# Convolution taps of three groups as matrices on TensorE, and five tiles' spikes as signs on ScalarE

## The chip, the cores and the metric

The kernel runs on one core of a Trainium2 chip. A core has TensorE (PE in the profile, its weight loads PEld), VectorE (DVE), ScalarE (ACT), GpSimdE (POOL) and SyncE (SP, which here issues the DMAs). TensorE writes its results to PSUM; the other operands lie in SBUF. The metric is device microseconds of one execution; smaller is better.

## The reference

The input is x, 16 sequences of 64 tokens with 256 features (1024 token rows), and a context of 16 x 1601 x 256. Six residual sublayers follow each other, each on a layer-normed x:

1. cross-attention over the context;
2. a selective state-space layer ("SSM"): in-projection, a causal convolution of four taps per channel, SiLU, projections to a step size delta and to b and c, a recurrence over the 64 tokens for 512 channels x 16 states, a gate, out-projection;
3. a spiking feed-forward layer;
4. windowed cross-attention over the context's first 64 rows;
5. a self-attention with a distance threshold;
6. a mixture of 8 experts with two chosen per token.

The change touches two places. The convolution, one filter of four taps for each of the 512 channels:

```python
xc = lax.conv_general_dilated(xc, conv_w, window_strides=(1,), padding=[(D_CONV - 1, 0)],
    dimension_numbers=('NCH', 'OIH', 'NCH'), feature_group_count=D_INNER)
xc = xc + conv_b[None, :, None]
x_b = jax.nn.silu(jnp.transpose(xc, (0, 2, 1)))
```

and the spikes of the feed-forward layer, five steps of a leaky integrator fed with the same y:

```python
reset = jax.lax.stop_gradient(spike_fn(mem - THRESHOLD))
mem_new = BETA * mem + y - reset * THRESHOLD
spk = spike_fn(mem_new - THRESHOLD)
...
return jnp.sum(spks, axis=0) / NUM_STEPS
```

Since y is the same in all steps, the number of spikes is a step function of y: it is the number of five thresholds (`SPIKES`, lines 110 to 136) that y lies above.

## The kernel before

The 1024 token rows are 8 tiles of 128 (two sequences each). Everything is float32.

The first part, sublayer 1 (`l0_cross`, line 545), goes through the tiles one after the other and reads the context: scores (line 609), exponentials, transposed weights (646, 651), weighted values (654).

The SSM goes by five groups of tiles, `GROUPS = [(0, 1), (1, 2), (3, 2), (5, 2), (7, 1)]`: first tile and number of tiles, so groups 0 and 4 have T = 128 token columns and groups 1, 2 and 3 have T = 256. It has two halves. `l0_ssm_prelude` (line 736) works with channels on the partitions: layer norm, then `project` for pairs of 128-channel chunks. For the first four chunks the in-projection lands in a PSUM bank, ScalarE writes it with its bias into a padded buffer `xpad` (line 776) and, times the last tap, into `ug` (line 782), and VectorE adds the three earlier taps, one instruction each (line 787). For the other four chunks (the gate) ScalarE only adds the bias (766). Then come SiLU (807, with a table load before and after it), x_proj (819), and in two halves the step size: dt matmuls (840), a softplus of several ScalarE, VectorE and GpSimd steps (846 to 866). delta, delta*u and b, c are written to DRAM (824, 868), from where `l0_ssm_state` reads them back spread over the partitions (893, 904).

`l0_ssm_state` (line 884) does 16 steps for a group, 80 in all: four ScalarE exponentials `decay` (922, two buffers), then on VectorE a product (942), a scan (943) and a product (944), then four TensorE matmuls with the matrix `fold` that sum over states (948). After each four steps comes a product with the gate (953), at the end the out-projection (`so_ps`) and its residual (373). Steps are counted here from 1 to 80 in program order: group 0 has steps 1 to 16, group 1 17 to 32, group 2 33 to 48, group 3 49 to 64, group 4 65 to 80.

The later sublayers go tile by tile in `later` (1649): `l0_ffn` (1028: fc and pj matmuls at the helper lines 438 and 448, spikes), `l1_cross` (1119), `l1_self` (1233), `l1_moe` (1398: hidden matmuls `he_ps`, outputs `eo_ps`, and on VectorE one weighted accumulation per expert at 1469). They run on streams with their own buffers and PSUM banks and overlap with the SSM of later tiles. Stream 3 and the preludes of groups 3 and 4 (`banks[: 1 if g >= P2 else 2]`, line 1560) share the PSUM bank "p".

For the spikes, `l0_ffn` copies the projection out of PSUM on ScalarE (1059), then VectorE compares it with the first threshold (1060) and adds the comparison with each of the four others (1062); the residual adds 0.2 times the count.

The order on each engine is fixed when the program is built: a list scheduler (`schedule_with_timeline_sim=True`, with costs from `scheduler_costs`, line 146) issues what its own model holds ready, by priority. Priorities come from offsets in the table `AT` (line 87), one for each block: 'C' for the cross-attention tiles, 'P' for the preludes, 'S' for the state halves, 'D' for the later sublayers of each tile, 'W' for weight loads. `HOLD = {4: (2, 2)}` keeps group 4's state half behind the self-attention of tile 2. Each engine then runs its list strictly in order.

Of the kernel before, what the change touches and what calls it, by code (L numbers as in the profile page):

```python
# [11 lines left out]
F32 = mybir.dt.float32  # L12
# [86 lines left out]
PB = 8  # L99
PADX, PADR, PADC, SPLD, SPLM = 1, 1, 1, 1, 1  # L100
VPV = 0
PAIR = 0
LNA = tuple(range(8))
ST1 = 1
# [114 lines left out]
def kernel(ctx: ExitStack, tc: tile.TileContext, a: dict, out: bass.AP):  # L219
# [486 lines left out]
    def l0_ssm_setup(w, pool, late):  # L706
        A.activation(w["am"], w["am"], AF.Exp)
        V.tensor_scalar(w["am"], w["am"], -1.0, None, ALU.mult)
        if CONV:
            w["taps"] = pool.tile([P, NE * DCONV, P], F32, name="taps")  # L710
            for c in range(NE):
                for t in range(DCONV):
                    V.tensor_scalar(
                        w["taps"][:, c * DCONV + t, :], ident, w["conv_w"][:, c, t : t + 1],
                        None, ALU.mult,
                    )

        w["b3"] = pool.tile([P, NE], F32, name="b3")
        V.tensor_mul(w["b3"], w["conv_w"][:, :, DCONV - 1], w["in_b"][:, 0:NE])
        V.tensor_add(w["b3"], w["b3"], w["conv_b"])  # L720
        w["xpad"] = []
        for k in range(2):
            t = pool.tile([P, GT // L, XP], F32, name=f"xpad{k}")
            G.memset(t, 0.0)
            w["xpad"].append(t)
        if DSK:
            w["Dd"] = late.tile([P, NE, P], F32, name="Dd")
            for c in range(NE):
                A.activation(w["Dd"][:, c, :], ident, AF.Copy, scale=w["D"][:, c : c + 1])
        w["decay"] = []  # L730
        for k in range(NDEC):
            t = late.tile([P, 4 * GT], F32, name=f"decay{k}")
            G.memset(t, 0.0)
            w["decay"].append(t)

    def l0_ssm_prelude(w, pp, late, banks, g):
# [22 lines left out]
        def project(oc):  # L759
            ps = bank("in_ps", [P, 2, T])  # L760
            for k in range(2):
                pe[g, "in", oc + k] = mm_T(ps[:, k, :], w["in_w"], hT, oc + k)
            if oc >= NE:
                for k in range(2):
                    c = oc + k
                    A.activation(
                        ug[:, c, :], ps[:, k, :], AF.Identity, bias=w["in_b"][:, c : c + 1]
                    )
                return
            xps = []  # L770
            for k in range(2):
                c = oc + k
                xp = w["xpad"][k][:, 0:nb, :]
                xps.append(xp)
                pv = ps[:, k, :].rearrange("p (b l) -> p b l", l=L)
                A.activation(
                    xp[:, :, DCONV - 1 :], pv, AF.Identity, bias=w["in_b"][:, c : c + 1]
                )
                if CONV:
                    continue  # L780
                cv = ug[:, c, :].rearrange("p (b l) -> p b l", l=L)
                A.activation(  # L782
                    cv, pv, AF.Identity, bias=w["b3"][:, c : c + 1],
                    scale=w["conv_w"][:, c, DCONV - 1 : DCONV],
                )
                for t in range(DCONV - 1):
                    V.scalar_tensor_tensor(  # L787
                        cv, xp[:, :, t : t + L], w["conv_w"][:, c, t : t + 1], cv,
                        ALU.mult, ALU.add,
                    )  # L790
# [32 lines left out]
        s["bc"] = dram.tile([2 * DST, T], F32, name=f"d_bc{g}")  # L823
        nc.sync.dma_start(out=s["bc"], in_=dbl[DTR:DBL, :])

        if split and not GLAST:
            for oc in range(NE, 2 * NE, 2):
                project(oc)


        s["delta"] = dram.tile([DIN, T], F32, name=f"d_delta{g}")
        s["du"] = dram.tile([DIN, T], F32, name=f"d_du{g}")
        for hf in range(2):
            shp = [P, 2, T]
            ps = bank("dt_ps", shp)
            e = sized(pp, "spe", 2, T)
            vp = sized(pp, "spv", 2, T, bufs=2)
            for k in range(2):
                c = 2 * hf + k
                pe[g, "dt", hf] = nc.tensor.matmul(  # L840
                    ps[:, k, :], w["dt_w"][:, c * P : (c + 1) * P], dbl if PADX else dbl[0:DTR, :],
                    start=True, stop=True,
                )
            for k in range(2):
# [21 lines left out]
            V.tensor_mul(du, vp, ug[:, 2 * hf : 2 * hf + 2, :])  # L866
            for k, t in (("delta", vp), ("du", du)):
                nc.sync.dma_start(
                    out=s[k].rearrange("(c p) t -> p c t", p=P)[:, 2 * hf : 2 * hf + 2, :],
                    in_=t,  # L870
                )
        if split:
            if GLAST:
                for oc in range(NE, 2 * NE, 2):
                    project(oc)
            with tc.issue_after(sp_last.ins) if SAFT else nullcontext():
                silu(ug[:, NE:, :])
        return s

    turns = [0]  # L880
# [3 lines left out]
    def l0_ssm_state(w, pp, s, g):  # L884
# [2 lines left out]
        x = xs[g]  # L887
        bc = []
        for q in range(2):
            t = sized(pp, f"bc{q}", 4, T)  # L890
            src = s["bc"][q * DST : (q + 1) * DST, :].rearrange("(k n) t -> n k t", n=SN)
            for n in range(SN):
                nc.sync.dma_start(
                    out=t[n * SD : (n + 1) * SD, :, :], in_=src[n].partition_broadcast(SD)
                )
            bc.append(t)
        yg = sized(pp, "yg", NE, T)
        for c in range(NE):
            rep = {}
            for k in ("delta", "du"):  # L900
                t = sized(pp, "rep_" + k, 4, T, bufs=REPB)
                src = s[k][c * P : (c + 1) * P, :].rearrange("(k d) t -> d k t", d=SD)
# [125 lines left out]
    def l0_ffn(w, st, i0):  # L1028
# [779 lines left out]
```

## Time and profile before

| | |
|---|---|
| median of 3 runs | 719.25 us (718.08 to 721.94) |
| the profiled execution | 717.57 us, span 715.5 us, mean granted TensorE clock 0.943 |
| TensorE busy | 616.6 us (86%) |
| VectorE busy | 520.0 us (73%) |
| ScalarE busy | 478.8 us (67%) |
| GpSimdE busy | 211.6 us (30%) |
| data moved by DMA | 102.56 MB |

Shares over the whole span hide that the stages have different limits. The first scan starts at 107.7 us; up to there TensorE and the DMA queues carry the cross-attention. Then VectorE carries the state steps, and from about 500 us on TensorE has hardly a gap. So times are read here by stretch: busy time of each engine between two events. A group of the profile (a "row") is all instructions of one line, operation and tile shape; it gives the busy time, the number and the mean duration. One float32 matmul of the program shows as two TensorE instructions in the profile.

### The profile page before, as it was taken

How to read it: one execution, taken by the hardware profiler on the slowest of the kernel's cores; microseconds unless marked ns; L12 is line 12 of the kernel's file. 1: busy time of each engine (PE TensorE's matmuls, PEld its weight loads, DVE VectorE, ACT ScalarE, POOL GpSimd, SP SyncE). 2: the span in 40 equal slices, each digit the busy share in tenths (PEclk: the TensorE clock that was granted, in tenths of full speed). 3: DMA queues.
4: the chain of work that ended last, by engine and by line, in shares of the span. 5: the costliest groups of instructions: out<-in, count | busy, mean ns of one | idle time of the engine just before them, and what ended most of it. 6: DMA issues, size and time to landing. Idle time of an engine off the chain costs nothing.

```text
span 715.5 us, 13023 instructions
## 1 busy us (share of the span) xinstructions
PE 616.6 (86%) x4508; PEld 436.3 (61%) x4508; DVE 520.0 (73%) x876; ACT 478.8 (67%) x1570; POOL 211.6 (30%) x300
## 2 busy tenths in 40 slices
PE   9988969989997487786786869789998989999997
PEld 7455545544653265553453647656787777878986
DVE  3424328896999999999999679999879944433432
ACT  3444536965677366797789667768977788674442
POOL 4110110130011579012226592522326533221100
PEclk9999998989999599899788789999999999999999
DMA  8999689799942954211113301255554540000000
GB/s 301 325 372 335 211 276 327 216 383 289 295 123 74 308 134 98 60 33 59 60 31 97 105 30 41 66 146 156 154 148 117 154 159 9 1 1 1 17 14 8
DMA packets 85383, 102.56 MB, mean 143 GB/s; under 512 B 11515, under 2 KB 67763, under 8 KB 85190
## 3 DMA queue, kind: packets, MB, share of 16 engines
q1 hardware_dynamic: 85318, 101.74, 46.2%
q8 instruction: 36, 0.59, 0.4%
q14 instruction: 29, 0.24, 0.1%
HBM read 96.33 MB, written 5.37 MB: 142 GB/s over the span
## 4 chain that ended last, share of the span: by engine, by line
PE 43%; DVE 24%; DMA 13%; ACT 8%; issue 6%; POOL 4%; SPq 2%; DVEq 0%; POOLq 0%; ACTq 0%
PE he_ps L438 7%; DVE hs L943 7%; PE eo_ps L448 6%; PE s_ps L609 6%; DVE hs L942 5%; DVE hs L944 4%; PE o_ps L654 4%; PE in_ps L438 3%; DMA w<-in_L_ffn_w 3%; ACT decay L922 2%; DMA rep_delta<-d_delta 2%; PE fc_ps L438 2%; DMA Wv<-in_L_attn_Wv 1%; DMA cT<-in_ctxT 1%; PE qk_ps L438 1%
## 5 line engine op out<-in xcount | busy, mean ns | idle before, releaser
L943 DVE TENSOR_TENSOR_SCAN hs<-decay,hs 128x1024 f32<-128x1024 f32 (+1 forms) x80 | 155.1, 1949 | 0.2
L922 ACT ACTIVATE decay<-rep_delta,ssm 128x252 f32<-128x252 f32 (+1 forms) x320 | 122.2, 458 | 37.8 <-DVE hs L943 30.5
L942 DVE TENSOR_TENSOR hs<-rep_du,bc 128x1024 f32<-128x1024 f32 (+1 forms) x80 | 87.9, 1106 | 14.1 <-PE y_ps L948 6.4
L944 DVE TENSOR_TENSOR hs<-hs,bc 128x1024 f32<-128x1024 f32 (+1 forms) x80 | 87.5, 1101 | 0.1
L948 PE MATMUL y_ps<-hs,fold 128*32 128x256 f32 (+1 forms) x640 | 45.3, 367 | 14.2 <-DVE hs L944 14.1
L609 PE MATMUL s_ps<-cT,qkT 128*64 128x512 f32 (+1 forms) x256 | 54.3, 509 | 0.4 <-ACT qkT L499 0.3
L1469 DVE SCALAR_TENSOR_TENSOR x<-eo_ps,pad,x 128x256 f32<-128x256 f32 x56 | 26.8, 478 | 37.5 <-PE eo_ps L448 37.4
L654 PE MATMUL o_ps<-cn,prT 128*64 128x256 f32 x384 | 51.0, 402 | 2.7 <-ACT prT L651 2.7
L1458 ACT ACTIVATE he<-he_ps,late 128x128 f32<-128x128 f32 x112 | 35.2, 366 | 24.7 <-PE he_ps L438 24.3
L1167 POOL TENSOR_TENSOR ke<-kT,hmask 128x512 f32<-128x512 f32 x28 | 45.7, 1651 | 15.7 <-PE s_ps L1172 15.2
L654 PEld LDWEIGHTS o_ps<-cn,prT 128*64 128x64 f32 x384 | 28.4, 144 | 21.4 <-ACT prT L651 5.9
L438 PE MATMUL in_ps<-hT,L_attn_in_proj_wT 128*128 128x256 f32 (+1 forms) x160 | 35.7, 374 | 5.9 <-ACT hT L432 4.6
L948 PEld LDWEIGHTS y_ps<-hs,fold 128*32 128x32 f32 x640 | 15.0, 112 | 35.7 <-DVE hs L944 21.6
L651 ACT COPY prT<-prT_ps 128x512 f32<-128x512 f32 (+1 forms) x32 | 16.1, 505 | 29.8 <-PE prT_ps L646 29.6
L438 PEld LDWEIGHTS in_ps<-hT,L_attn_in_proj_wT 128*128 128x128 f32 x160 | 28.3, 214 | 12.3 <-ACT hT L432 4.7
L1179 ACT ACTIVATE sm<-s_ps,wmx 128x64 f32<-128x64 f32 x112 | 33.6, 322 | 3.2 <-DVE wmx L1176 3.1
L438 PE MATMUL fc_ps<-hT,L_ffn_W_fcT 128*128 128x128 f32 x224 | 29.9, 284 | 6.2 <-ACT hT L432 6.2
L438 PEld LDWEIGHTS fc_ps<-hT,L_ffn_W_fcT 128*128 128x128 f32 x224 | 27.8, 196 | 8.9 <-ACT hT L432 7.3
L438 PE MATMUL he_ps<-hT,w 128*128 128x128 f32 x192 | 27.3, 284 | 6.4 <-DMA w<-in_L_ffn_w 3.9
L627 POOL TENSOR_TENSOR xnb<-xmx,qb 128x1 f32<-128x1 f32 x8 | 2.7, 334 | 101.4 <-DVE xmx L616 88.1
L787 DVE SCALAR_TENSOR_TENSOR ug<-xpad,ssm,ug 128x256 f32<-128x256 f32 (+1 forms) x60 | 26.2, 461 | 8.2 <-ACT ug L782 7.8
L609 PEld LDWEIGHTS s_ps<-cT,qkT 128*64 128x64 f32 x256 | 17.0, 136 | 23.8 <-issue 18.4
(406 smaller groups left out, 1495.2 us busy)
## 6 DMA issues: line engine op xcount, KB each, us to landing
cn<-in_ctx SPq DMA_DIRECT2D x48, 512.0 KB
cT<-in_ctxT SPq DMA_DIRECT2D x42, 512.0 KB
w<-in_L_ffn_w SPq DMA_DIRECT2D x48, 256.0 KB
rep_delta<-d_delta SPq DMA_DIRECT2D x48, 128.0 KB
rep_du<-d_du SPq DMA_DIRECT2D x48, 128.0 KB
bc<-d_bc SPq DMA_DIRECT2D x24, 128.0 KB
rep_delta<-d_delta SPq DMA_DIRECT2D x32, 64.0 KB
rep_du<-d_du SPq DMA_DIRECT2D x32, 64.0 KB
```

What stands on the lines that cost most here:

```text
L438: last = nc.tensor.matmul(ps, w[:, kc, oc * P : (oc + 1) * P], src[:, kc, :], start=(kc == 0), stop=(kc == nk - 1),)
L448: nc.tensor.matmul(ps, srcT[:, kc, j * P : (j + 1) * P], w[:, kc, :], start=(kc == 0), stop=(kc == nk - 1),)
L609: nc.tensor.matmul(s_ps[r * L : (r + 1) * L, :n], q["qkT"][:, kc, r * L : (r + 1) * L], cT[r][:, kc, :], start=(kc == 0), stop=(kc == KC - 1),
L654: q["last"] = nc.tensor.matmul(q["o"][r * L : (r + 1) * L, :], prT[:n, j % 4, r * L : (r + 1) * L], cn[r, j], start=(j == 0), stop=(j == NKB),
L922: A.activation(dav[:, (4 * j + k) * nb : (4 * j + k + 1) * nb, 1:], rep["delta"][:, k, :].rearrange("p (b l) -> p b l", l=L)[:, :, 1:], AF ...
L942: V.tensor_mul(hv, dv, bv)
L943: V.tensor_tensor_scan(hf, da, hf, 0.0, ALU.mult, ALU.add)
L944: V.tensor_mul(hv, hv, cv)
L948: nc.tensor.matmul(y_ps[k * SD : (k + 1) * SD, :], fold, hs[:, 4 * j + k, :], start=(m0 + j == 0 and not DSK), stop=(m0 + j == NG - 1),)
L1167: G.tensor_mul(ke, kT[:, c, tok].unsqueeze(1).to_broadcast([P, HPC, L]), hmask.unsqueeze(2).to_broadcast([P, HPC, L]),)
L1179: A.activation(sm[:, k, :], s_ps[:, k, :], AF.Exp, bias=nmx[:, k : k + 1], accum_out=su[i][:, c * HPC + k : c * HPC + k + 1],)
L1458: A.activation(he[:, oc, :], ps[:, oc, :], AF.Relu, bias=w["b1"][:, e * KC + oc : e * KC + oc + 1],)
```

## The change

- `CVG = (2, 3, 4)`: in these groups' preludes line 782 and the three VectorE taps of line 787 are left out. Instead ScalarE builds four 128x128 matrices for each chunk, the identity times one tap's column of weights (48 instructions in all; they lie in the buffers `spe` and `spd` of the softplus), TensorE multiplies them with four shifted views of `xpad` and sums in a bank `cv_ps` (48 matmuls), and ScalarE writes that with the convolution's bias into `ug`.
- `SPKA = (0, 1, 2, 3, 4)`: for these tiles the copy and the five VectorE instructions are left out. ScalarE takes the sign of y minus each threshold as bfloat16 straight from PSUM (5 instructions), TensorE adds the five signs and a half with the identity (6 matmuls in bfloat16), and ScalarE turns the sum into a whole count in two instructions, adding and subtracting 3 * 2**22.
- Constants for this: 8 GpSimd memsets near the start.
- All offsets in `AT` are replaced.
- `PR = ()` brings a further variant that is not used (no group is in it). A DMA of `bc` is put behind that condition and otherwise unchanged.

```diff
-AT = {'C': [-2353, 5581, 7142, -5613, 8966, 8274, 4756, 5756], 'P': [8396, -16035, 6317, -7280, -4284], 'S': [-14451, -3588, 2275, 4502, 10207], 'D': [1074, 3097, 6442, 3653, 3047, 2495, 11233, 1972, 3894, 14390, 5543, -1098, -3696, 8030, 8748, 8626, 4822, -6980, 6568, -2434, 5400, 13909, -16420, 15355, 10997, 6273, 17387, 6006, 5142, 8066, 4192, 8614], 'W': [22978, 1143]}
+AT = {'C': [-5139, 6805, 7005, -2417, 3697, 7786, 3506, 9074], 'P': [7946, -18619, 10584, -6550, -1170], 'S': [-13797, -4499, 733, 6029, 9327], 'D': [1201, 2427, 8508, 2754, 4728, 3096, 9632, 3223, 5211, 22017, 5232, -2472, -6148, 9346, 9404, 9102, 4452, -7971, 6779, -1693, 3783, 14663, -19173, 10370, 11088, 4756, 17922, 6455, 6997, 8294, -28, 9918], 'W': [14796, -151]}
...
+CVG = (2, 3, 4)
+SPKA = (0, 1, 2, 3, 4)
+PR = ()
...
+    c_spk = cpool.tile([P, len(SPIKES)], F32, name="c_spk")
+    for k, v in enumerate(SPIKES):
+        G.memset(c_spk[:, k : k + 1], -v)
+    c_rnd = cpool.tile([P, 2], F32, name="c_rnd")
+    G.memset(c_rnd[:, 0:1], 2.0 + 3.0 * 2**22)
+    G.memset(c_rnd[:, 1:2], -3.0 * 2**22)
+    halfb = cpool.tile([P, 1], BF16, name="halfb")
+    G.memset(halfb, 0.5)
...
-                if CONV:
+                if CONV or g in CVG:
                     continue
...
+            if g in CVG:
+                ps = bank("cv_ps", [P, 2, T])
+                for k in range(2):
+                    taps = sized(pp, ("spe", "spd")[k], DCONV, P, most=P)
+                    for t in range(DCONV):
+                        A.activation(
+                            taps[:, t, :], ident, AF.Copy,
+                            scale=w["conv_w"][:, oc + k, t : t + 1],
+                        )
+                    for t in range(DCONV):
+                        nc.tensor.matmul(
+                            ps[:, k, :], taps[:, t, :], xps[k][:, :, t : t + L],
+                            start=(t == 0), stop=(t == DCONV - 1),
+                        )
+                for k in range(2):
+                    c = oc + k
+                    A.activation(
+                        ug[:, c, :], ps[:, k, :], AF.Identity, bias=w["conv_b"][:, c : c + 1]
+                    )
...
-        if i0 in SPKB:
+        if i0 in SPKA:
+
+
+            sums = st.bank("spk_ps", shp)
+            for k, v in enumerate(SPIKES):
+                r = st.new("r", [P, nt * D // 2]).bitcast(BF16).rearrange("p (n d) -> p n d", n=nt)
+                A.activation(r, ps, AF.Sign, bias=c_spk[:, k : k + 1])
+                nc.tensor.matmul(sums, identb, r, start=(k == 0), stop=False)
+            nc.tensor.matmul(
+                sums, identb, halfb.unsqueeze(1).to_broadcast(shp), start=False, stop=True
+            )
+            total = st.new("total", shp)
+            A.activation(total, sums, AF.Identity, bias=c_rnd[:, 0:1], scale=0.5)
+            A.activation(total, total, AF.Identity, bias=c_rnd[:, 1:2])
+        elif i0 in SPKB:
```

The lists of instructions that the build gives differ, besides the order, only by these numbers: VectorE has 36 taps and 25 spike instructions fewer; ScalarE has 48 taps, 25 signs and 10 rounding steps more and 5 copies fewer (12 instructions of line 782 become 12 of the new bias line); TensorE has 48 float32 and 30 bfloat16 matmuls more; GpSimd has 8 memsets more. The DMAs are the same, in another order.

More of the change, by code (lines that the diff above doesn't have):

```diff
@@ L729, in l0_ssm_setup @@
                 A.activation(w["Dd"][:, c, :], ident, AF.Copy, scale=w["D"][:, c : c + 1])
+        if PR:
+            t = late.tile([P, 4 * GT], F32, tag="bc0", name="seld")
+            w["bc0"] = t[:, 0 : 4 * P].rearrange("p (k t) -> p k t", k=4)
+            w["seld"] = t[:, 4 * P :].rearrange("p (k t) -> p k t", k=4)
+            w["selb"] = sized(late, "hs", 8, P, bufs=HSB, most=P)
+            for j in range(4):
+                G.tensor_copy(
+                    w["seld"][:, j, :].rearrange("p (n d) -> p n d", d=SD),
+                    ident[:, j * SD : (j + 1) * SD].unsqueeze(1).to_broadcast([P, SN, SD]),
+                )
+            for k in range(8):
+                r = DTR + k * SN
+                G.tensor_copy(
+                    w["selb"][:, k, :].rearrange("p (n d) -> p n d", d=SD),
+                    ident[:, r : r + SN].unsqueeze(2).to_broadcast([P, SN, SD]),
+                )
         w["decay"] = []
@@ L789, in project @@
                         ALU.mult, ALU.add,
+                    )
[12 more added lines that the diff above has]
+                            start=(t == 0), stop=(t == DCONV - 1),
+                        )
+                for k in range(2):
+                    c = oc + k
+                    A.activation(
+                        ug[:, c, :], ps[:, k, :], AF.Identity, bias=w["conv_b"][:, c : c + 1]
                     )
@@ L822, in l0_ssm_prelude @@
         A.copy(dbl, ps)
-        s["bc"] = dram.tile([2 * DST, T], F32, name=f"d_bc{g}")
-        nc.sync.dma_start(out=s["bc"], in_=dbl[DTR:DBL, :])
+        if g not in PR:
+            s["bc"] = dram.tile([2 * DST, T], F32, name=f"d_bc{g}")
+            nc.sync.dma_start(out=s["bc"], in_=dbl[DTR:DBL, :])
         if split and not GLAST:
@@ L828, in l0_ssm_prelude @@
                 project(oc)
-        s["delta"] = dram.tile([DIN, T], F32, name=f"d_delta{g}")
-        s["du"] = dram.tile([DIN, T], F32, name=f"d_du{g}")
+        s["rep"] = []
+        if g not in PR:
+            s["delta"] = dram.tile([DIN, T], F32, name=f"d_delta{g}")
+            s["du"] = dram.tile([DIN, T], F32, name=f"d_du{g}")
         for hf in range(2):
@@ L866, in l0_ssm_prelude @@
             V.tensor_mul(du, vp, ug[:, 2 * hf : 2 * hf + 2, :])
+            if g in PR:
+                s["rep"] += [(vp[:, k, :], du[:, k, :]) for k in range(2)]
+                continue
             for k, t in (("delta", vp), ("du", du)):
@@ L877, in l0_ssm_prelude @@
                 silu(ug[:, NE:, :])
+        if g in PR:
+            s["bc"] = []
+            for q in range(2):
+                t = sized(late, "bc1", 4, T) if q else w["bc0"]
+                ps = bank("bc_ps", [P, 4, T])
+                for k in range(4):
+                    nc.tensor.matmul(
+                        ps[:, k, :], w["selb"][:, q * 4 + k, :],
+                        dbl, start=True, stop=True,
+                    )
+                A.copy(t, ps)
+                s["bc"].append(t)
+        s["bank"] = bank
         return s
@@ L889, in l0_ssm_state @@
         for q in range(2):
+            if g in PR:
+                bc.append(s["bc"][q])
+                continue
             t = sized(pp, f"bc{q}", 4, T)
@@ L901, in l0_ssm_state @@
                 t = sized(pp, "rep_" + k, 4, T, bufs=REPB)
+                if g in PR:
+                    ps = s["bank"]("rep_ps", [P, 4, T])
+                    for j in range(4):
+                        nc.tensor.matmul(
+                            ps[:, j, :],
+                            w["seld"][:, j, :],
+                            s["rep"][c][k == "du"], start=True, stop=True,
+                        )
+                    A.copy(t, ps)
+                    rep[k] = t
+                    continue
                 src = s[k][c * P : (c + 1) * P, :].rearrange("(k d) t -> d k t", d=SD)
@@ L1043, in l0_ffn @@
         shp = [P, nt, D]
-        if i0 in SPKB:
+        if i0 in SPKA:
[4 more added lines that the diff above has]
+                nc.tensor.matmul(sums, identb, r, start=(k == 0), stop=False)
+            nc.tensor.matmul(
+                sums, identb, halfb.unsqueeze(1).to_broadcast(shp), start=False, stop=True
+            )
+            total = st.new("total", shp)
+            A.activation(total, sums, AF.Identity, bias=c_rnd[:, 0:1], scale=0.5)
+            A.activation(total, total, AF.Identity, bias=c_rnd[:, 1:2])
+        elif i0 in SPKB:
             y = st.new("y", shp)
```

## The prediction

> **What bounds the kernel now.** I read the busy slices first, then busy times by stretch, then VectorE's rows and waits, then the order of the instructions.
>
> ```profile
> PE   9988969989997487786786869789998989999997
> DVE  3424328896999999999999679999879944433432
> ACT  3444536965677366797789667768977788674442
> PEclk9999998989999599899788789999999999999999
> ```
>
> VectorE is full from about 180 to 500 us; TensorE has gaps there and none behind. Two events part the stretches: the first scan (107.7 us) and the scan of step 61 (480.9 us), whose fold matmuls end at 489.8 us.
>
> ```profile
> 0.00:107.70 107.70, 93.55 (x630) 59.04 (x630) 35.79 (x109) 47.35 (x122) 17.62 (x62) 0.97 0.91 303
> 107.70:480.90 373.20, 299.90 (x2115) 193.95 (x2119) 346.41 (x467) 271.14 (x813) 130.42 (x131) 0.90 0.48 142
> 480.90:715.50 234.60, 223.13 (x1767) 183.27 (x1759) 137.84 (x303) 160.28 (x638) 63.60 (x108) 1.00 0.25 73
> 489.80:715.50 225.70, 214.99 (x1706) 178.53 (x1706) 128.94 (x288) 153.83 (x612) 62.45 (x105) 1.00 0.24 71
> ```
>
> Columns after the length: busy TensorE, weight loads, VectorE, ScalarE, GpSimd, then TensorE's clock. In the second stretch VectorE is idle for 26.8 us, TensorE for 73.3, ScalarE for 102.1: VectorE sets its length. Behind step 61 TensorE is idle for 10.7 of 225.7 us: TensorE sets the end. What VectorE is spared therefore pays only by letting this dense part begin earlier, and whatever TensorE is given to do there comes off.
>
> VectorE's rows that the change takes from, and its waits in the second stretch:
>
> ```profile
> L787 DVE SCALAR_TENSOR_TENSOR ug<-xpad,ssm,ug 128x256 f32<-128x256 f32 x36 | 17.6, 506 | 1.9 <-ACT ug L782 1.7
> L787 DVE SCALAR_TENSOR_TENSOR ug<-xpad,ssm,ug 128x128 f32<-128x128 f32 x24 | 8.6, 393 | 6.3 <-ACT ug L782 6.2
> L1062 DVE SCALAR_TENSOR_TENSOR total<-y,total 128x256 f32<-128x256 f32 x28 | 14.8, 529 | 0.1
> L1060 DVE TENSOR_SCALAR total<-y 128x256 f32<-128x256 f32 x7 | 2.8, 405 | 1.7 <-ACT f L1038 1.0 <-ACT y L1059 0.8
> ```
>
> ```profile
> DVE hs L942 <- DMA rep_delta<-d_delta: 6.0, 1, 6.0
> DVE hs L942 <- PE y_ps L948: 4.7, 4, 2.7
> DVE few L1362 <- ACT sm L1357: 4.1, 1, 4.1
> DVE ug L787 <- ACT ug L782: 1.7, 1, 1.7
> DVE total L1060 <- ACT f L1038: 1.0, 1, 1.0
> ```
>
> **The change, part by part.** I price by a row's busy time over its number.
>
> *VectorE, second stretch.* Removed: 24 taps at 17.6/36 = 0.489 us (11.7), 12 at 8.6/24 = 0.358 (4.3), 20 comparisons at 14.8/28 = 0.529 (10.6), 5 at 0.4 (2.0): 28.6 us. The new order moves more: adding row prices over VectorE's list from the first scan to that of step 61 gives 378.1 us before and 336.4 after, 41.7 less. So 13.1 us of other work (four expert accumulations of line 1469, residuals, small steps of the self-attention) now stand behind step 61. Rows overlap: 378.1 stand for 346.4 busy, so 336.4 stand for 308.2.
>
> *Waits.* Of 26.8 us idle, 1.7 and 1.0 belong to removed instructions. 4.1 is a reciprocal for which VectorE waits on ScalarE at 406 to 410 us; in the new list a gate product, two products and a scan stand between the reduction ahead of it and that reciprocal, which cover the wait. I leave 20.0. Ends: 0 (no wait left) and 53.6 (twice the row, ScalarE and TensorE both being fuller); I take 20.0, since the four large waits that stay have causes that are untouched. Step 61's scan then starts at 107.7 + 308.2 + 20.0 = 435.9 instead of 480.9, its folds end at 444.8.
>
> *TensorE ahead of step 61.*
>
> ```profile
> L438 PE MATMUL in_ps<-hT,L_attn_in_proj_wT 128*128 128x256 f32 x96 | 25.3, 412 | 5.3 <-ACT hT L432 4.6 <-ACT ug L782 0.6
> L438 PE MATMUL in_ps<-hT,L_attn_in_proj_wT 128*128 128x128 f32 x64 | 10.5, 318 | 0.6 <-ACT ug L782 0.6
> L1158 PE MATMUL s_ps<-cneg,identb 128*64 128x512 bf16 x32 | 6.7, 415 | 0.7 <-DVE qu L1136 0.7
> ```
>
> A float32 matmul is two records: 25.3/48 = 0.527 us and 10.5/32 = 0.328. The taps cost 32 x 0.527 + 16 x 0.328 = 22.1 us, all ahead of step 61. A bfloat16 spike matmul of half the row's width lies between 0.1 and 0.21 (half the row, the row); 30 cost 3.1 to 6.3, I take 3.1, as matmul rows here shrink with width. Yet TensorE's list ahead of step 61's folds, from the first fold on, falls from 317 to 298 us of row prices: at the old ratio to busy (299.8/317) 282 us in some 329, 86% against 80%. The 22.1 us are hidden by TensorE's idle time; without that cover they come on top.
>
> *TensorE behind step 61.* Instead of 910 matmuls 1062 follow: 32 more expert hidden and 14 output matmuls, 12 fc, 10 pj, 12 for spikes and the attention of later tiles. By rows 263 become 311 us; 263 stood for 215.0 busy, so 311 stand for 254.1, 39.1 more. Nothing hides these. Idle stays 10.7.
>
> *ScalarE.*
>
> ```profile
> L729 ACT ACTIVATE Dd<-ident,ssm x4: 385/386/388, 38.2 to 39.1; 128x128 f32<-128x128 f32 x4
> L766 ACT ACTIVATE ug<-in_ps,ssm 128x256 f32<-128x256 f32 x12 | 5.0, 469 | 5.8 <-PE in_ps L438 5.8
> ```
>
> 48 taps at 0.386 are 18.5 us; 25 signs and 10 rounding steps at 0.469 are 16.4; five copies go (-1.9), line 782's successor is cheaper (-1.1): 31.9 us. ScalarE's list up to step 61 stays at 294 us of rows, since other work moves behind it: 271 busy in 328 instead of 373, 83% instead of 73%. I price this at nothing on the path, covered by its idle time; without cover it is the second rival. Both lists have 11 table loads (1.283 us each in the profile), so the signs bring none.
>
> [...]
>
> *The rest.* Eight memsets (0.1 us in their row's size) come early on GpSimd; the loads of the context (3.7 to 10.5 us) and x (10.5 to 17.2) cover them, else +0.8. In groups 3 and 4 the single bank "p" now holds also the taps' sums, 8 x 0.527 = 4.2 us more per pair; the prelude of group 3 spent 282 to 306 us, mostly queued behind scans, so this is no longer than before. The DMAs are the same number; in SP's list group 2's writes of delta and du and its first reads now stand ahead of the feed-forward weights. Those were issued from 232 us on and fc began at 297, so they can wait for some tens of us.
>
> *Sum.* 444.8 + 254.1 + 10.7 = 709.6 us span, 2.1 around it: **711.7, say 712**, against 717.57 of the profiled execution (its median is 1.7 above). VectorE gives 45, TensorE's longer list takes 39.
>
> **The rivals.**
>
> *Faster still (700).* VectorE's waits go to 8 and nothing else changes. For: 200 to 400 us had 4 us of waits in all. Against: the waits on DMA (6.0) and on folds (4.7) have untouched causes.
>
> *Slower: ScalarE is late with the decays (726).* Between the scans ScalarE's queue now holds runs of eight taps (3.1 us, six of them) and of five signs with two roundings (3.3 us, three tiles ahead of step 61): 28.4 us, each in front of some decay that has only two buffers. If VectorE waits for half, step 61 comes 14 us later and the end at 726. It decides from 9.5 us of such waits on (721). For: ScalarE rises to 83%. Against: decays waited 30.5 us for scans, so ScalarE was ahead.
>
> *Slower: group 2's round trip (722).* By rows there are 19 us between the last product of its first half and step 33 (42 before); the slowest trip in the chain of waits took 18 us (147.1 to 165.4). A queue in front, like the 10.6 us of a weight load there, makes step 33 late by 10. Against: these weights now go behind it.
>
> *No gain (718).* TensorE can't do 282 us of mixed work in 329, and step 61 is 6 us later. Against: the 282 are counted at the old stretch's clock of 0.90, and behind 490 us it is 1.00.
>
> [...]
>
> **How the numbers follow.** My sum 0.50 (own range 704 to 720), 700 0.18, ScalarE's lateness 0.18, the round trip 0.06, no gain 0.08. The ends of the waits give 692 and 745. Below 697 VectorE would have to wait for under 5 us in all, above 730 for over 38; a tenth each, so 697 to 730. Under 0.5% (3.6 us) this kernel can't be told from unchanged: from 714 to 721 is the same. Of my sum 0.31 is faster, 0.14 the same, 0.05 slower; with the rest faster 0.50, same 0.24, slower 0.26.
>
> **What would show it.** Right: the 61st scan near 436 us, VectorE's idle time from the first scan to it near 20, TensorE busy some 254 of 265 us behind its folds, he_ps and eo_ps among them. Wrong: large waits of hs (943) on decay (922); a wait of line 942 on DMA before step 33; TensorE idle more than 20 us behind step 61; taps or signs far from 0.386 and 0.469.

## The result and the profile after

The changed kernel takes 741.85 us (median; 740.91 to 742.60), the kernel before 718.92 in the same series: a ratio of 1.031 [1.028, 1.034], slower by 3%. 712 was forecast, with 697 to 730 as the range; the time lies outside it and on the other side. The profiled execution took 742.03 us with a span of 740.3. In the table of the experiments one execution each of both_old and both_pfree, in which the chip was in a slower state, is left out of the median and the ratio.

The busy slices of the changed kernel:

```profile
PE   9998999769896878977997867899998999999997
DVE  2433369598799895899999996845889225334332
```

The stretches in the form of the table of before (length; busy time of TensorE, weight loads, VectorE, ScalarE, GpSimd; granted clock), from the first scan (101.4 us) to the scan of step 61 (459.1), and from the end of step 61's folds (467.0) to the end:

```profile
101.40:459.10 357.70, 293.69 (x1999) 189.61 (x1996) 311.65 (x361) 264.44 (x774) 107.93 (x108) 0.87 0.49 145
467.00:740.30 273.30, 257.72 (x1988) 212.87 (x1986) 135.42 (x336) 184.41 (x732) 66.47 (x128) 0.99 0.24 72
```

Step 61 comes 21.8 us earlier than before (480.9), not 45. The part behind its folds grows from 225.7 to 273.3 us. The difference of the spans is 467.0 - 489.8 + 273.3 - 225.7 = 24.8 us. In the first stretch VectorE's idle time is 357.70 - 311.65 = 46.05 us, where 20 were forecast and 26.8 stood before. TensorE is busy there for 82%, with gaps.

VectorE's largest waits in that stretch, and the rows of the new operations:

```profile
DVE hs L1024 <- PE y_ps L1030: 11.5, 7, 4.4
DVE diff L1406 <- POOL few L1398: 5.9, 1, 5.9
DVE yg L1035 <- PE y_ps L1030: 5.0, 4, 3.7
DVE hs L1024 <- DMA bc<-d_bc: 5.0, 1, 5.0
DVE hs L1024 <- DMA rep_du<-d_du: 4.7, 2, 4.5
```

```profile
L1133 ACT ACTIVATE r<-pj_ps,c_spk 128x256 bf16<-128x256 f32 x25 | 9.8, 491 | 1.7 <-PE pj_ps L460 1.7
L825 ACT ACTIVATE spe<-ident,ssm 128x128 f32<-128x128 f32 x24 | 7.6, 389 | 2.0 <-PE cv_ps L830 2.0
L830 PE MATMUL cv_ps<-xpad,spd 128*128 128x256 f32 x32 | 7.9, 383 | 0.0
L1134 PE MATMUL spk_ps<-r,identb 128*128 128x256 bf16 x25 | 4.9, 272 | 1.9 <-ACT r L1133 1.3
```

Of the kernel before, the prediction shows the products' wait for folds (`y_ps`), 4.7 us, but not that of the product with the gate:

```profile
DVE yg L953 <- PE y_ps L948: 3.5, 1, 3.5
```

The waits for folds have grown from these 4.7 and 3.5 us to 11.5 and 5.0; none is a wait of a scan or product for a decay. The rows of matrices, signs and tap matmuls are close to the prices of the prediction (a float32 tap matmul, two records, takes 7.9/16 = 0.494 us for 0.527). The bfloat16 spike matmul is not: 4.9/25 = 0.196 us, where 0.1 was taken.

### The profile page after: what moved, and what is told of

Same layout as the page of the kernel before. It is cut to its first block, busy times and chain, and to the rows that moved or that the text cites. A ratio compares the mean times of both kernels' runs of the same rounds, so it can differ in the third digit from the quotient of the medians.

```text
span 740.3 us, 13311 instructions
## 1 busy us (share of the span) xinstructions
PE 650.9 (88%) x4634; PEld 465.8 (63%) x4634; DVE 490.7 (66%) x815; ACT 501.8 (68%) x1648; POOL 193.8 (26%) x308
## 5 line engine op out<-in xcount | busy, mean ns | idle before, releaser
L1025 DVE TENSOR_TENSOR_SCAN hs<-decay,hs 128x1024 f32<-128x1024 f32 (+1 forms) x80 | 152.6, 1913 | 1.1
L666 PE MATMUL o_ps<-cn,prT 128*64 128x256 f32 x384 | 54.9, 407 | 5.7 <-ACT prT L663 5.7
L1030 PE MATMUL y_ps<-hs,fold 128*32 128x256 f32 (+1 forms) x640 | 48.7, 381 | 10.6 <-DVE hs L1026 10.6
L1263 POOL TENSOR_TENSOR ke<-kT,hmask 128x512 f32<-128x512 f32 x28 | 41.1, 1489 | 21.0 <-PE s_ps L1268 20.7
L666 PEld LDWEIGHTS o_ps<-cn,prT 128*64 128x64 f32 x384 | 30.7, 143 | 22.5 <-ACT prT L663 7.9
L450 PE MATMUL fc_ps<-hT,L_ffn_W_fcT 128*128 128x128 f32 x224 | 34.8, 304 | 0.8 <-ACT f L1120 0.5
L450 PEld LDWEIGHTS fc_ps<-hT,L_ffn_W_fcT 128*128 128x128 f32 x224 | 31.9, 216 | 5.4 <-issue 1.3
L621 PEld LDWEIGHTS s_ps<-cT,qkT 128*64 128x64 f32 x256 | 17.9, 139 | 26.8 <-issue 21.4
L639 POOL TENSOR_TENSOR xnb<-xmx,qb 128x1 f32<-128x1 f32 x8 | 4.6, 578 | 106.5 <-DVE xmx L628 58.4
L460 PE MATMUL pj_ps<-L_ffn_W_projT,f 128*128 128x256 f32 x112 | 28.6, 400 | 2.0 <-ACT f L1121 1.0
```

The lines of the kernel that those rows point to most:

```text
L450: last = nc.tensor.matmul(ps, w[:, kc, oc * P : (oc + 1) * P], src[:, kc, :], start=(kc == 0), stop=(kc == nk - 1),)
L460: nc.tensor.matmul(ps, srcT[:, kc, j * P : (j + 1) * P], w[:, kc, :], start=(kc == 0), stop=(kc == nk - 1),)
L621: nc.tensor.matmul(s_ps[r * L : (r + 1) * L, :n], q["qkT"][:, kc, r * L : (r + 1) * L], cT[r][:, kc, :], start=(kc == 0), stop=(kc == KC - 1),
L666: q["last"] = nc.tensor.matmul(q["o"][r * L : (r + 1) * L, :], prT[:n, j % 4, r * L : (r + 1) * L], cn[r, j], start=(j == 0), stop=(j == NKB),
L1025: V.tensor_tensor_scan(hf, da, hf, 0.0, ALU.mult, ALU.add)
L1030: nc.tensor.matmul(y_ps[k * SD : (k + 1) * SD, :], fold, hs[:, 4 * j + k, :], start=(m0 + j == 0 and not DSK), stop=(m0 + j == NG - 1),)
```

## The experiments

Steps are counted as before. In the expectations, "operations", "offsets" and "order" are three theories of the loss: the added instructions, the particular offsets of the new `AT`, or any list that the scheduler makes anew. All ratios are to the kernel before, run on the same chip in turn with each kernel.

| kernel | median, us | ratio [95%] |
|---|---|---|
| none_old | 764.83 | 1.063 [1.058, 1.067] |
| none_new | 764.23 | 1.062 [1.058, 1.066] |
| both_old | 755.54 | 1.049 [1.044, 1.053] |
| taps_old | 777.89 | 1.078 [1.072, 1.084] |
| none_held | 718.50 | 0.999 [0.996, 1.002] |
| both_held | 732.62 | 1.020 [1.016, 1.025] |
| taps_held | 737.51 | 1.028 [1.023, 1.032] |
| signs_held | 715.24 | 0.996 [0.994, 0.999] |
| taps_one | 728.46 | 1.016 [1.011, 1.021] |
| taps_ident | 730.29 | 1.017 [1.012, 1.022] |
| taps_g2 | 722.07 | 1.005 [1.002, 1.008] |
| taps_g34 | 730.10 | 1.015 [1.007, 1.023] |
| none_pfree | 722.57 | 1.007 [1.004, 1.010] |
| both_slow | 751.96 | 1.047 [1.042, 1.053] |
| both_pfree | 733.73 | 1.022 [1.017, 1.027] |
| none_aorder | 750.51 | 1.047 [1.042, 1.052] |
| relief_taps | 714.78 | 0.994 [0.990, 0.997] |
| relief_both | 709.67 | 0.989 [0.982, 0.996] |

### Edits and offsets apart

The changed kernel with its two edits switched off (the eight constants stay), with the offsets of before or of after; then both edits, or the taps alone, with the offsets of before.

```diff
-CVG = (2, 3, 4)
-SPKA = (0, 1, 2, 3, 4)
+CVG = ()
+SPKA = ()
-AT = {'C': [-5139, 6805, 7005, -2417, 3697, 7786, 3506, 9074], 'P': [7946, -18619, 10584, -6550, -1170],
+AT = {'C': [-2353, 5581, 7142, -5613, 8966, 8274, 4756, 5756], 'P': [8396, -16035, 6317, -7280, -4284],
...
```

none_old:

> The changed kernel with both edits off (no group's taps on TensorE, no tile's signs on ScalarE) and the offsets of before: the instructions of before plus 8 GpSimd memsets of 0.1 us. Theory 'operations' (what was moved to TensorE and ScalarE costs more than VectorE is spared): 719 us, as before. Theory 'offsets' (the replaced table AT costs the time): 719 as well. Theory 'order' (the list order of before was fitted to exactly that program, and any program that the scheduler orders anew loses it): its TensorE list has 297 us of row prices behind step 61's folds against 263 before, so 731 to 750 us.

none_new:

> Both edits off, with the new offsets. Theory 'operations': 719 us. Theory 'offsets': 742, the whole loss. Theory 'order': 728 to 747, from VectorE's list up to step 61 (370 us of row prices) and 289 us of TensorE behind it.

both_old:

> Both edits on, with the offsets of before. Theory 'operations': 742 us, as after. Theory 'offsets': 719 or less. Theory 'order': 709 to 728, from 338 us of VectorE rows up to step 61 and 301 of TensorE behind it.

taps_old:

> The taps on TensorE alone, offsets of before. Theory 'operations': the taps bring 22.1 of 25 us of TensorE's new work, so 736 us. Theory 'offsets': 719 or less. Theory 'order': 715 to 734, from 352 us of VectorE rows and 293 of TensorE behind step 61.

All four are far above 719. none_old has before's instructions and offsets and eight memsets of 0.1 us more, and yet takes 46 us longer. Eight instructions more are enough for the scheduler to make other lists. Among the three with before's offsets, both edits are 9 us faster than none and the taps alone 13 slower, which lists and edits can each explain. So a comparison in which the scheduler orders anew mixes the price of the edits with that of the lists.

### Before's lists, held

To part the two, the following kernels force each engine's list by edges of issue order alone (none_held, which has before's lists in full, takes 0.999 of the time of before):

```diff
+def hold_order(tc):
...
+    for e, code in HELD.items():
+        order = np.cumsum(np.frombuffer(zlib.decompress(base64.b85decode(code)), np.int16).astype(int))
+        for a, b in zip(order, order[1:]):
+            tc.add_manual_dep(
+                by[e][b], by[e][a].name,
+                mybir.DependencyInfo(mybir.DependencyClass.NoSync, mybir.DependencyReason.DATA),
+                reason="held",
+            )
...
         tile_perceiver_kernel(tc, aps, out)
+        hold_order(tc)
```

`HELD` holds before's place of every instruction that both programs have. none_held is none_old with these edges; taps_held has `CVG = (2, 3, 4)` alone, signs_held `SPKA = (0, 1, 2, 3, 4)` alone, both_held the two. Where there are taps, the instructions of the prelude's own lines are left to the scheduler, while the in-projection matmuls, issued by a helper, are held. In taps_held, besides the taps, mainly ScalarE's writes of `xpad` and 16 of TensorE's records of x_proj then stand elsewhere in their lists; what this costs by itself was not measured.

> The instructions of before and the eight constants, with before's list on every engine forced by edges of issue order alone (an engine's instruction k+1 behind its k); only the eight memsets of 0.1 us stand in addition, early on GpSimd. 'Order' (the 45 us of the run without edits at before's offsets come from the lists that the scheduler made anew): 719, at most 722. 'Constants' (the memsets, or the memory that the constants take, cost them): about 760 again. If it is neither, between 725 and 755, the forcing itself costs something.

> Both edits, with before's list on every engine for all instructions that both programs have, outside the preludes; new instructions and the preludes' own are put between them by the scheduler. TensorE's list behind step 61 is then that of before, save spike matmuls of tile 4. 'Relief' (VectorE sets the stretch, as the prediction said; what is spared passes to the end when the list behind is not longer): 28.6 us of taps and comparisons less, TensorE's 22 us hidden, 719 - 28.6 + about 1 = 691, range 685 to 705. 'TensorE' (the 22 us of tap matmuls are not hidden in the stretch): 691 + 22 = 713. 'Edits cost' (round trips from ScalarE over TensorE to ScalarE keep the engines waiting, whatever the order): 735 or more.

> The tap matrices alone, before's list held outside the preludes. 'Relief': 16.0 us of VectorE's taps less, 719 - 16 = 703. 'TensorE': 703 + 22 = 725. 'Edits cost': 730 or more, if the taps are what costs.

> The signs alone, before's list held everywhere. 'Relief': 12.6 us of VectorE's comparisons less, of which some 10 ahead of step 61: 719 - 10 = 709 (706 to 714). 'TensorE': the 30 bfloat16 matmuls are 8 us of records at 0.27 us: 714 to 719. 'Edits cost': 725 or more, if the signs are what costs.

"Order" holds: 718.5 with held lists, 764.8 without, for the same instructions. The constants cost nothing. With held lists the signs gain 0.4%, 3 us of the 10 of "relief"; 715.2 lies in the range of "TensorE" (714 to 719). The taps lose 2.8%, which goes to "edits cost" (730 or more). Both lose 2.0%: 732.6 is far above "TensorE" (713) and just under "edits cost" (735). So of the 23 us of the change about 14 stand against both edits in before's order and 9 against the new lists. (A later run, none_aorder, shows that counting the other way round gives another split.)

Where the taps lose time is seen first around step 17 of taps_held. There TensorE was full before (the kernel before's stretch from step 17 to step 21, in the form of the tables above):

```profile
180.00:207.00 27.00, 25.84 (x183) 15.84 (x181) 26.52 (x41) 19.30 (x41) 1.61 (x3) 1.00 0.92 261
```

The same steps of taps_held:

```profile
178.00:213.00 35.00, 33.84 (x216) 22.87 (x215) 22.47 (x30) 22.57 (x49) 1.49 (x3) 1.00 0.67 206
```

TensorE's work grows by 8.0 us and so does the stretch, while VectorE's falls by 4.1. TensorE's list of taps_held there (start, length, line, tiles, number):

```profile
182.63 1.97 PE L852 MATMUL cv_ps<-xpad,spe 128*128 128x256 f32 x8 [0.66 <-ACT xpad L827]
184.43 1.89 PE L852 MATMUL cv_ps<-xpad,spd 128*128 128x256 f32 x8
...
188.77 1.99 PE L852 MATMUL cv_ps<-xpad,spe 128*128 128x256 f32 x8 [0.50 <-ACT xpad L827]
190.60 1.89 PE L852 MATMUL cv_ps<-xpad,spd 128*128 128x256 f32 x8
...
194.60 0.61 PE L1052 MATMUL y_ps<-hs,fold 128*32 128x256 f32 x8
```

and VectorE's next product:

```profile
195.29 1.23 DVE L1046 TENSOR_TENSOR hs<-rep_du,bc 128x1024 f32<-128x1024 f32 x1 [8.38 <-DMA rep_delta<-d_delta]
```

The fold of step 17 stood at 187.68 us before; here four runs of tap matmuls, 7.6 us, are ahead of it, and VectorE stands idle for 8.38 us. The trace puts this wait down to a DMA, but the product starts 0.1 us after the fold ends (194.60 + 0.61), and in taps_one (the next section) the wait at the same place is put down to the fold.

Over the whole stretch from the first scan to step 61, taps_held has:

```profile
107.00:499.10 392.10, 318.73 (x2201) 210.92 (x2200) 330.47 (x430) 282.64 (x849) 124.75 (x130) 0.90 0.44 134
```

Against the kernel before, TensorE's busy time grows by 18.8 us (from 299.90) and the stretch by 18.9 (from 373.20). TensorE's idle time stays at 73.4 us, where 73.3 stood: in this order it hid none of the new work.

### What of the taps costs

taps_one makes one of the four matmuls of each chunk, taps_ident builds no matrices; taps_g2 and taps_g34 have taps in group 2 alone and in groups 3 and 4 alone. All in before's order.

```diff
-                    for t in range(DCONV):
+                    for t in (DCONV - 1,):
                         nc.tensor.matmul(
                             ps[:, k, :], taps[:, t, :], xps[k][:, :, t : t + L],
-                            start=(t == 0), stop=(t == DCONV - 1),
+                            start=True, stop=True,
                         )
```

```diff
-                    taps = sized(pp, ("spe", "spd")[k], DCONV, P, most=P)
...
-                            ps[:, k, :], taps[:, t, :], xps[k][:, :, t : t + L],
+                            ps[:, k, :], ident, xps[k][:, :, t : t + L],
```

> As the tap matrices alone in before's order (737.5), but of the four tap matmuls of each chunk only the last is made; three of four products of the convolution are left out, all 48 matrices are still built by ScalarE. 'TensorE' (the tap matmuls' own time in front of folds and scores is the cost): 33 of 48 matmuls with 15 us of records go, so about 737 - 15 to 20 = 717 to 723. 'ScalarE' (48 matrices of 0.386 us in front of the decays, or the trip from ScalarE over TensorE back to ScalarE): 732 or more.

> As the tap matrices alone in before's order, but all 48 matmuls multiply with the identity that is there anyway; the 48 scaled matrices are left out, so ScalarE is spared 18.5 us and the convolution's weights are left out. 'TensorE': 733 to 738, unchanged. 'ScalarE': 719 or less.

> Tap matrices for group 2 alone, before's order. In the trace with all three groups TensorE is 97% busy from step 17 to step 21, the folds of step 17 stand behind 7.6 us of tap matmuls, and VectorE waits 8.4 us there. 'Full stretch' (the taps cost what they take where TensorE is full, VectorE's 5.9 us are lost in waits): 719 + 8 = 727, with step 21 at 213 us. 'Relief': 713.

> Tap matrices for groups 3 and 4 alone, before's order. There TensorE is some 75% busy from 280 to 394 us. If only the full stretch of group 2 costs ('full stretch'), the rest is hidden and VectorE's 10.2 us come back: 709 to 715. If each tap matmul in front of a fold or a score that VectorE waits for costs its time ('in front of folds', whatever TensorE's mean share): 725 to 732, with step 45 some 10 us later than before.

Neither "TensorE" nor "ScalarE" alone fits: three quarters of the matmuls give back 9 us of the 19, the matrices 7 (both against 737.5, in another series). (The text of taps_one speaks of 33 matmuls fewer; with one of four kept, 36 of 48 go.) A further part may lie in the idle time in front of the tap matmuls, until `xpad` is written (us, times), first taps_held:

```profile
  ACT xpad L827: 15.4, 7
```

and taps_one:

```profile
  ACT xpad L827: 21.4, 7
```

In a strict list TensorE stands at the tap matmuls until ScalarE has written `xpad`, with folds and scores queued behind. With fewer matmuls it stands longer. VectorE's wait behind step 17 shrinks in taps_one only from 8.38 to 7.12 us; ahead of that fold TensorE stands idle for 2.77 us at the tap matmuls, for `xpad`:

```profile
193.13 1.23 DVE L1046 TENSOR_TENSOR hs<-rep_du,bc 128x1024 f32<-128x1024 f32 x1 [7.12 <-PE y_ps L1052]
```

Before, the taps were on VectorE and TensorE's list did not meet `xpad` at all. The exact split between work, wait and matrices stays open.

taps_g2 has step 21 at 211 us, 207 before; 213 was forecast. It loses only 3 us at the end, not 8: its first scan comes 2.7 us earlier (105.0), and counted from there step 21 is 6.3 us later than before, step 61 4.0. taps_g34 agrees with "in front of folds" in place and size (step 45 at 375 us against 367 before, where some 10 us were forecast; 1.5% [0.7, 2.3] at the end), though TensorE's mean share there is 75%.

### Another place for the tap matmuls, and before's program in after's order

both_slow tries to put the tap matmuls behind the wait: the scheduler's model gets 3 us more for the write of `xpad`, and the prelude's whole function is free of the held order. both_pfree is the same without the 3 us, none_pfree the control without edits. none_aorder has before's instructions in after's lists.

```diff
+                if g in CVG:
+                    LATE_NS[i.ins.name] = 3000
...
     def longer(ins, ns):
+        ns += LATE_NS.get(ins.name, 0)
```

> No edit; before's list held on every engine for all instructions outside the prelude's function, the prelude's own placed by the scheduler. The control for the two runs below: 719, at most 724 if the freed placement is worse.

> Both edits, before's order outside the prelude's function; in the scheduler's own model the write of xpad in groups 2 to 4 lasts 3 us longer, so the tap matmuls stand later in TensorE's list (behind the folds of one step more), with no instruction added. 'Wait in the list' (TensorE, standing at the tap matmuls for ScalarE's xpad, holds up the folds and scores behind it, 10.3 us in the run with both edits in before's order): 732.6 - 8 = 725, or less, with under 4 us of idle time ahead of cv_ps. 'Work' (the matmuls' own 18 us are the cost wherever they stand): 730 to 734.

> As the run before it without the 3 us: the in-projection and tap matmuls stand where the scheduler's unchanged model puts them. 'Wait in the list': 730 to 733, with some 10 us of idle time ahead of cv_ps. 'Work': 730 to 734.

> The instructions of before in the order of after (outside the prelude's function; VectorE's and ScalarE's own spike instructions of tiles 0 to 4 placed by the scheduler). 'New lists' (the order of after is worse by itself, by what it costs against both edits in before's order, 742 - 733 = 9 us): 719 + 9 = 728. 'Fitted' (that order is good for the edited program alone, and any other program in it is slower): 745 or more.

Freeing the prelude costs 0.7% by itself. both_slow misses badly: 752. The idle time ahead of the tap matmuls is still 11.6 us, and VectorE's products wait 22.9 us for folds, where 15.8 stood in both_held. So whether a good place exists in this order is not shown; this one is none. both_pfree, at 733.7, doesn't part the two readings (730 to 733 and 730 to 734). Against its own control, none_pfree, the edits cost it 11 us.

none_aorder goes to "fitted": 750.5. The edits save about 9 us in after's lists (742 against 751) and cost 14 in before's. Counted this way round, the new lists cost some 33 us (750.5 against 717.4 in its series) and the edits give 9 back, so the split into 14 and 9 is no property of the edits. The spike instructions and the preludes of none_aorder were placed by the scheduler, so this holds for lists and placement together.

From the first scan to step 61 none_aorder has:

```profile
101.90:464.50 362.60, 271.07 (x1885) 168.49 (x1880) 329.34 (x411) 245.18 (x706) 108.48 (x108) 0.86 0.48 143
```

VectorE is idle for 33.3 us here, without either edit, where 26.8 stood before. Two of the three largest waits of the changed kernel that are not for folds stand here as well (line 1046 is the product), and the third, for `bc`, with 2.9 us:

```profile
DVE diff L1428 <- POOL few L1420: 5.9, 1, 5.9
DVE hs L1046 <- DMA rep_du<-d_du: 4.5, 1, 4.5
```

They come with the lists. The edits take 17.7 us from VectorE's busy time (329.34 to 311.65) and add 12.8 to its idle time (33.3 to 46.05), so step 61 comes only 5.4 us earlier (459.1 for 464.5).

### VectorE's work taken away, nothing in its place

In before's lists, relief_taps leaves out VectorE's 36 taps, relief_both also 20 comparisons.

```diff
-                for t in range(DCONV - 1):
+                for t in range(0 if g >= 2 else DCONV - 1):
...
-            for v in SPIKES[1:]:
+            for v in SPIKES[1:] if i0 > 4 else ():
```

> The kernel before with all lists held, only that the 36 VectorE taps of groups 2 to 4 are left out (the convolution's earlier three taps are missing there) and nothing takes their place. 'VectorE sets the stretch' (the prediction's premise): 16.0 us of rows, so 719 - 16 = 703, with step 61 at 465 us. 'Shared' (at most places another engine is as late, TensorE above all, and VectorE only waits longer): 711 or more. The distance to the tap matrices in the same order (737.5) is what the operations in their place cost.

> As the run before it, and the 20 comparisons behind the first of tiles 0 to 4 are left out too (the count then tells only the first threshold). 'VectorE sets the stretch': 16.0 + 10.6 us of rows, 719 - 26.6 = 692, step 61 near 455 us. 'Shared': 706 or more, with VectorE's waits in the stretch above 40 us.

This tests the premise of the prediction, and the premise falls: 0.64% [0.3, 1.0] and 1.13% [0.4, 1.8], 5 and 8 us, for 16.0 and 26.6 us of rows. From the first scan to step 61, first none_held (full work, held lists):

```profile
106.90:481.00 374.10, 300.33 (x2119) 193.85 (x2119) 346.83 (x467) 271.43 (x817) 130.67 (x131) 0.90 0.48 141
```

then relief_taps and relief_both:

```profile
106.00:476.00 370.00, 300.95 (x2115) 194.17 (x2119) 333.13 (x431) 271.56 (x814) 125.62 (x131) 0.91 0.48 143
```

```profile
105.00:470.00 365.00, 299.62 (x2110) 193.32 (x2111) 326.59 (x410) 270.42 (x809) 131.35 (x131) 0.90 0.48 145
```

VectorE's busy time falls by 13.7 and 20.2 us, its idle time rises from 27.3 to 36.9 and 38.4. Over half of what VectorE is spared comes back as its own waiting. Both times go to "shared" (711 or more, 706 or more), though relief_both's idle time stays just under the 40 us given there. The waits that grow, none_held and then relief_taps:

```profile
DVE hs L1046 <- PE y_ps L1052: 4.6, 4, 2.5
...
DVE pr L650 <- PE s_ps L643: 2.3, 3, 1.6
```

```profile
DVE hs L1046 <- PE y_ps L1052: 10.2, 9, 2.9
DVE pr L650 <- PE s_ps L643: 5.8, 3, 3.8
```

They are waits for folds and scores, both TensorE's. In relief_taps those of more than 1 us that none_held doesn't have stand at five places between 200 and 307 us.

## Why the prediction was wrong

The steps of the sum, against the measured ones: the first scan came 6.3 us earlier (101.4 for 107.7, not foreseen); VectorE's busy time in the stretch was right (311.65 for 308.2); its waits were 46.05 for 20.0; step 61's folds ended 7.9 us behind its scan for 8.9; TensorE's busy time behind them was right within 1.5% (257.72 for 254.1), its idle time 15.6 for 10.7. The deviations, -6.3 + 3.4 + 26.1 - 1.0 + 3.6 + 4.9, are the 30.7 us between the span forecast (709.6) and the one measured (740.3). One term carries it.

**The step that failed** is "I take 20.0, since the four large waits that stay have causes that are untouched". It treats waits as a fixed remainder. In the changed kernel VectorE's busy time fell by 34.8 us and its idle time rose by 19.3, 55% of it; the two relief runs, with unchanged lists, show 70% and 55%. The reason behind it is the reading "VectorE sets its length": true of the sum over 373 us, not of every part. At steps 17 to 21 TensorE was 96% busy as well (25.84 of 27.00 us), and the relief runs have new waits for folds and scores at other places too. The 26.1 us that the term was short have two parts of like size. 13.3 stand in none_aorder already (33.3 for 20.0): waits that the new lists make, for `few` on GpSimd and for reads of `rep_du` and `bc`, although their causes seemed untouched. 12.8 come with the edits, against 17.7 us of VectorE's work that they spare. The upper end that was given for the waits, 53.6, would have held the 46, but the range stopped counting at 38.

One of the lines behind that term was misread: the wait of 6.0 us for `rep_delta` ends at 106.5 us, ahead of the first scan (107.7), and is no part of the stretch. The 20.0 don't change by it, as the 26.8 they start from were counted without it; but it is not one of the "four large waits that stay".

**The cover that failed in one order** is "The 22.1 us are hidden by TensorE's idle time". That TensorE's 73 us of gaps could take the tap matmuls holds as a sum, but in before's order not in place: there the taps cost 19 us although VectorE was spared 16. Part of it may be TensorE's new wait for `xpad` (15.4 us), which the prediction did not name: it looked at who waits for ScalarE's decays, not at what is queued behind the first tap matmul in TensorE's list. In the changed kernel's own lists the cover is not shown to have failed. That wait is 1.3 us there, and against none_aorder TensorE is busy for 22.6 us more in the stretch (293.69 for 271.07), yet step 61 comes earlier.

**What was right:** the prices on ScalarE (taps 0.389 us against 0.386, signs 0.491 against 0.469), and TensorE's longer list behind step 61, which was to take 39 of VectorE's 45 us. It took 43 in busy time (257.72 - 214.99), and as VectorE gave 22, it decided the sign.

**The rivals:** lateness of ScalarE's decays did not come; no wait for a decay stands in VectorE's list. The round trip of group 2 left no large wait on a DMA ahead of step 33, which came at 267 us, 13 earlier than before. The two large waits on DMAs stand elsewhere: 4.5 us at 134 us, in group 0, and 5.0 at 284 us, behind the scan of step 34. "No gain" named TensorE, which was busy for 293.7 us in the stretch and not 282 (at a clock of 0.87, not 0.90), but it put step 61 only 6 us later than the sum, and 23 were measured. None of the rivals' times reaches the one measured.

The spikes' move from VectorE to ScalarE (0.529 and 0.405 us a comparison, 0.491 us a sign) is in before's order a gain of 0.4% [0.1, 0.6], small but no loss. The granted clock in the stretch was 0.87 with TensorE 82% busy, where before had 0.90 at 80%. Counting gaps between matmuls doesn't settle why: in the whole execution the changed kernel has 13 of over 2 us and the one before 8, but of over 4 us 2 and 5. Why its clock is lower stays open.

The fastest kernel of the study that does the whole work is signs_held, 715.24 us: the signs alone, in before's lists, just below the kernel before.

## What to carry to other kernels

An engine that is 93% busy over a long stretch is not its only bound: before counting its relief as gain, look for the parts where a second engine is as full, and take the work away with nothing in its place and the order unchanged; here some 30% of the rows' time reached the end (4.6 of 16.0 us, 8.1 of 26.6). Where a program is ordered by a list scheduler, compare edits with held lists, since the order can be worth more than the edit: here 46 us, where the signs gained 3. And when work moves to an engine with a strict list, price what stands behind its first wait there, not only its busy time; here TensorE stood idle for 15.4 us at the tap matmuls until `xpad` was written (taps_held).

## What the runs showed of the hardware

The same 4508 TensorE records cost 617.3 us in none_held and 637.7 in none_old, by order alone; 224 matmuls of fc take 29.8 us in the one and 34.5 in the other. The granted clock goes with it: 0.942 in the mean of the one, 0.911 in the other. From 400 to 500 us, none_held and then none_old:

```profile
400.00:500.00 100.00, 81.61 (x601) 59.19 (x599) 89.43 (x129) 71.45 (x253) 46.52 (x56) 0.95 0.31 87
```

```profile
400.00:500.00 100.00, 72.67 (x571) 51.08 (x570) 92.23 (x117) 70.05 (x256) 57.69 (x66) 0.80 0.16 43
```

In these runs the order that leaves TensorE more idle (27 us of the 100, against 18) is also the one with the lower clock (0.80 against 0.95) and the longer matmuls (34.5 against 29.8 us for those of fc). Whether the idle time lowers the clock no run tested by itself.
